# The two score rounds of a key block pair issued together in the middle steps of a four-layer kernel

## The chip, the core and the metric

The kernel runs on one core of a Trainium2 chip. The metric is the device time of one execution in microseconds (us). The times of before are those of 11 runs; the profile is one further execution of the same program, recorded by the hardware profiler.

## The reference, cut to what matters

Four layers are added to x one after another. x has B = 8 sequences of S = 256 tokens of D = 256 numbers. The change concerns the two attention layers, of 16 heads of 16 numbers each.

```python
# layer 0: x = x + (attention and SwiGLU, each behind a conditioned RMS norm)
x = x + _attention(_tc_rmsnorm(x, t, g1w, g1b, b1w, b1b), Wq, Wk, Wv, Wo)
return x + _swiglu(_tc_rmsnorm(x, t, g2w, g2b, b2w, b2b), gate_w, hid_w, out_w)
# attention, in both layer 0 and layer 1 (layer 1 has a mask)
attn = einsum('blhd,bmhd->bhlm', q, k) / scale
p = softmax(attn, axis=-1)
o = einsum('bhlm,bmhd->blhd', p, v)
return o @ Wo.T
# layer 1: attention, RMS norm of its output, a shift and scale from the condition
# layer 2: a quaternion rotation of x3 (in the kernel: products with coefficients)
# layer 3: a mixture of 8 experts, 2 for each token, chosen by a router
```

## The kernel before, in words

All matmuls are fp32, and every instruction of TensorE (PE) stands in the order in which the text of the kernel issues it; in the middle part the instructions of VectorE (DVE) and ScalarE (ACT) do so too (`manual_schedule`). Nothing is moved by a scheduler there.

**Rounds.** `Attention` works on one sequence in one layer. Its heads come in KC = 2 groups c of 8 heads, and the keys in NQ = 2 blocks kc of 128. `scores(c, kc)` (L988) multiplies 4 row tiles of 32 into one score tile `s_a` of 128 x 2048 numbers, and ACT writes its exponential into `pe_a` (L990). `values(c)` (L1001) multiplies both exponentials of a group with the values `va` into `o_a`, in column tiles of 32; DVE then turns and divides the result (`tu_a`, `invs`, `on_a`, `oT_a`, L1010 to L1018). `block()` issues one round: the scores, and then the values of the group whose two exponentials are complete, if one is waiting in `pending`. So an even round (kc = 0) issues scores and values, an odd round (kc = 1) scores alone.

**Pieces.** Between the rounds stand pieces of other work, taken from a generator (`others`), each about 1.7 us of matmuls: the chunks of SwiGLU (`pg`, `ph`, L1128; `pd`, L1141), the projections of the next attention (`pk_a`, `pq_a`, L932; `pv_a`, L954 and L962), transposes (`pt_n`, `pt_x`, L888), and the outward projections (`py`, L1024 and L1174). A `pg` is followed on ACT by the tanh `th` (L1132) and on DVE by `sg` (L1134); a `ph` by `hT` on DVE (L1136); a `pd` reads `hT`.

**PSUM.** The score tile has one buffer, the value tile one, and all the pieces share three:

```python
ps_m = banks.enter_context(tc.tile_pool(name="ps_m", bufs=3, space=PSUM))      # L532
ps_s = last_rounds.enter_context(tc.tile_pool(name="ps_s", bufs=1, space=PSUM))  # L534
ps_o = last_rounds.enter_context(tc.tile_pool(name="ps_o", bufs=1, space=PSUM))  # L535
```

The pieces' buffers are taken in turn: py takes over that of `pg_0`, `ph_2` that of `ph_0`, `pg_4` that of `pg_2`, `ph_4` that of py, and so on. `pe_a` has three buffers.

**Steps.** The loop `for i in range(2, B - 1)` makes five middle steps. Step i calls `run("bbbbbbbb", ...)`: eight rounds, four of layer 1 of sequence i - 2 and four of layer 0 of sequence i + 1, with the pieces of `others(i - 1)`. `run` holds the order: after round t it first starts the generators in `starts[t]`, then takes pieces until the time of `gaps` is spent (in the text's own units), with the outward projection of a finished attention (`then`) among them, and at the end of the round the generators in `beside[t]`. These put work on DVE and ACT: the norms' squares (L878, L1225, ACT) and reciprocal roots (`rsqrt`, L619 to L624, DVE), `xs_n` (L900, ACT), the rotation (L1202, L1207), and, in steps 4 and 6, the routing of a group of two sequences (`route`, L1236 to L1278; `place_choices`). The scores of the next attention read `qz_a` (L946, DVE) and `kT_a` (L942, ACT).

After the loop come the last rounds, with pieces of the first expert tiles, and then the experts by themselves (L1528, L1558).

Of the kernel before, what the change touches and what calls it, by code (L numbers as in the profile page):

```python
# [17 lines left out]
B, S, D = 8, 256, 256  # L18
# [475 lines left out]
def block_kernel(ctx: ExitStack, tc: tile.TileContext, a: dict, out: bass.AP):  # L494
# [372 lines left out]
    def wt(tag, shape, name, bufs=None):  # L867
        return homes.get(tag, work).tile(shape, F32, tag=tag, bufs=bufs or 2, name=name)
# [104 lines left out]
    class Attention:  # L973
# [19 lines left out]
        def values(self, c):  # L993
            va = self.ops[2]
            o = ps_o.tile([P, 2, S], F32, tag="o", name=f"o_{self.name}_{c}")
            for kc in range(NQ):
                pe = self.pes.pop((c, kc))

                for qd in range(2):
                    for i in range(4):  # L1000
                        nc.tensor.matmul(  # L1001
                            o[32 * i : 32 * i + 32, qd, :],
                            va[:, kc, 8 * c + 4 * qd + i].rearrange("p a d -> p (a d)"),
                            pe[:, 2 * qd + i // 2, i % 2, :],
                            start=kc == 0 and qd == 0, stop=kc == NQ - 1 and qd == 1,
                        )


            turned = wt("oS", [P, 2, S // 32, 2, DH], f"tu_{self.name}_{c}")
            nc.vector.transpose(turned.rearrange("p q j a d -> p (q j a d)"), o.rearrange("p q s -> p (q s)"))  # L1010
            inv = invs[:, self.at + c]
            nc.vector.reciprocal(inv, turned[:, :, :, 1, 0])
            on = wt("on", [P, S // 32, 2, DH], f"on_{self.name}_{c}")
            nc.vector.tensor_tensor(
                on.rearrange("p j q d -> p q j d"), turned[:, :, :, 0, :],
                inv.unsqueeze(3).to_broadcast([P, 2, S // 32, DH]), ALU.mult,
            )
            nc.vector.transpose(self.oT[:, c, :], on.rearrange("p j q d -> p (j q d)"))  # L1018
# [13 lines left out]
    def do_deferred():  # L1032
        while deferred:
            for _ in deferred.pop(0):
                pass
# [5 lines left out]
    def in_parts(b, key):  # L1041

        yield from state[b].pop(key)
# [150 lines left out]
    def rotate(b):  # L1194

        g, bi = divmod(b, GB)
        x3 = state[b].pop("x3").rearrange("p t (i c) -> p t i c", c=C)
        x4, raw = groups[g]
        dst = x4[:, bi * NQ : (bi + 1) * NQ, :].rearrange("p t (j c) -> p t j c", c=C)
        for i in range(4):  # L1200
            term = wt("oS", [P, NQ, 4, C], f"term_{b}_{i}") if i else dst
            nc.vector.tensor_tensor(  # L1202
                term, x3[:, :, i, :].unsqueeze(2).to_broadcast([P, NQ, 4, C]),
                coef[:, i].unsqueeze(1).to_broadcast([P, NQ, 4, C]), ALU.mult,
            )
            if i:
                nc.vector.tensor_tensor(dst, dst, term, ALU.add)  # L1207
            if i in (1, 2):
                yield
        if bi == GB - 1:  # L1210
            x4, raw = groups.pop(g)
            for o in (tokens_r, out_r):
                nc.sync.dma_start(out=o[:, g * NTG : (g + 1) * NTG, :], in_=x4)
        yield
        if bi == GB - 1:
            yield from route(g, x4, raw)
# [473 lines left out]
    def block():  # L1690
        layer, b, c, kc = queue.pop(0)
        second = layer == "a1"
        if (c, kc) == (0, 0):
            live[layer, b] = Attention(
                state[b].pop(f"qkv{int(second)}"), f"{layer}_{b}", (2 * b + second) * KC
            )
        live[layer, b].scores(c, kc)
        then = values()
        if second and (c, kc) == (KC - 1, NQ - 1):
            nc.vector.tensor_copy(wo1[:, :, D:], hall[:, :, b, :])  # L1700
        if kc == NQ - 1:
            pending.append((layer, b, c))
        return then

    def run(what, pieces, us=0.0, beside={}, rest=True, owed=None, hold=False, soon=3, late_=(), starts={}):

        spent, due, held = 0.0, 0.0, None
        for t, kind in enumerate(what):
            then = block() if kind == "b" else values() if kind == "v" else None
            do_deferred()
            for g in starts.get(t, ()):
                next(g, None)
            if held:
                held()  # L1720
                spent += 1.9
            held = None
            then, owed = then or owed, None
            if t in late_:
                held, then = then, None
            gap = us if isinstance(us, float) else us[t]
            due = max(due + gap, spent + min(gap, 3.0))
            n = 0
            while spent < due or (then and n < soon):
                w = next(pieces, "end")  # L1730
                if w == "break":
                    due = spent
                if w in ("break", "end"):
                    break
                spent += 1.9 if w is None else w
                n += 1
                if then and n == soon:
                    then()
                    spent += 1.9
                    then = None  # L1740
            if then and hold:
                return then
            if then:
                then()
                spent += 1.9
            for g in beside.get(t, ()):
                next(g, None)
        if rest:
            for _ in pieces:
                pass  # L1750
# [5 lines left out]
    def of(f, b):  # L1756
        return f(b) if 0 <= b < B else iter(())
# [3 lines left out]
    def others(b):  # L1761


        nxt, mine = of(first, b + 3), swiglus.pop(b)
        swiglus[b + 1] = of(swiglu, b + 1)
        n = 0 if b == 0 else 1
        for k, w in enumerate(mine, n):
            yield w
            if k == 0:
                yield "break"  # L1770
            if k == 11:

                yield next(nxt) if b + 3 < B else next(swiglus[b + 1], 0.0)
            if k == 12:
                if b + 3 < B:
                    yield next(nxt)
                    yield next(nxt)
                else:
                    yield "break"
            if k == 13:  # L1780
                if b + 3 < B:
                    yield from nxt
                else:
                    yield "break"
            if k == 14 and b + 3 < B:
                yield next(swiglus[b + 1])

    def once(f, *args):
        f(*args)
        yield  # L1790

    def at_once(*gens):
        for g in gens:
            for _ in g:
                pass
        yield
# [10 lines left out]
    with tc.manual_schedule(engines=by_text):  # L1807
# [35 lines left out]

        operands = first(1)
        run("b", chain(take(1, operands), set_up_condition(), set_up_router(cond_g)), 9.0, rest=False)
        run("b", take(1, operands), 9.0, {0: [once(prepare_quaternions)]}, rest=False)
        n1 = first_norm(2)
        run("b", iter(()), 0.0, {0: [n1]})
        run("b", operands, 9.0, {0: [at_once(n1)]}, rest=False)
        operands = first(2)  # L1850
        then = run("b", iter(()), 0.0, hold=True)
# [23 lines left out]
        gaps = [1.9, 5.0, 7.2, 7.2, 7.2, 7.2]  # L1875
# [5 lines left out]
    for i in range(2, B - 1):  # L1881

        placed = {
            2: lambda: once(compare_queries), 3: lambda: once(set_up_rows), 4: lambda: at_once(place_choices(0)),
            6: lambda: at_once(place_choices(1)),
        }.get(i, lambda: iter(()))()
        last, rotated = rotated, rotate(i - 2)
        n1 = first_turned(i + 2) if i + 2 < B else iter(())
        n2, r1 = in_parts(i, "n2"), in_parts(i - 2, "r1")
        gaps = [7.6, 5.7, 3.8, 5.7, 8.2, 3.8, 2.5, 3.8] if i + 2 < B else [7.6, 3.8, 1.9, 5.7, 7.6, 1.2, 1.9, 3.8]  # L1890
        starts = {0: [last, n1], 1: [last, n2], 2: [n2]}
        beside = {
            0: [last, n1], 1: [last, n2], 2: [n1], 3: [last], 4: [placed], 5: [r1], 6: [rotated],
            7: [rotated, rotated],
        }
        if i == B - 2:

            early = table("early", (NG - 2) * NTG, EARLY, ALU.is_ge)
            beside[4].insert(0, early)
            beside[7].append(early)  # L1900
        run("bbbbbbbb", others(i - 1), gaps, beside, late_=() if i + 2 < B else (4,), starts=starts)


    pieces = others(B - 2)
# [20 lines left out]
    pieces = last  # L1925
# [22 lines left out]
    owed = block()  # L1948
# [162 lines left out]
```

## Time and profile before

| | |
|---|---|
| median of 11 runs | 703.74 us |
| lowest and highest | 702.47 and 706.68 us |
| the profiled execution | 703.11 us |
| its span, first to last instruction | 701.3 us |
| mean granted TensorE clock in it | 0.997 |
| the five middle steps in it | 92.08 to 355.25 us |
| lengths of the steps i = 2 to 6 | 53.16, 53.17, 54.21, 53.17, 49.46 us |
| scores, all 64 rounds | 73.0 us of PE |
| exponentials, 64 | 120.1 us of ACT, 1877 ns each |

A step is counted from the start of its first scores to the start of the next step's first scores. PE's busy time is that of matmuls; PEld is the loading of weights, which runs beside them. In the lists of the chain and the timeline, the first number is the start and the second the length in us, and in square brackets stands the idle time before, with what ended it. An end of a matmul in the profile is modelled, so lengths on PE are best read from start to start.

### The profile page before, as it was taken

Reading aid. Unit: us, or ns where it says so; the run is one execution under the profiler, and the core shown is the slowest. Engines: PE = TensorE matmul, PEld = TensorE weight load, DVE = VectorE, ACT = ScalarE, POOL = GpSimd, SP = SyncE. Lnnn points to the kernel's source line nnn. Section 1 sums busy time; section 2 is a strip of 40 time slices with the busy share of each in tenths; the row PEclk is TensorE's granted clock in tenths of the full one; section 3 lists DMA queues with packets and bytes.
Section 4 is the critical chain, followed back from the end, with each engine's and each line's share of the span. In section 5 each row is a group of like instructions: output and inputs, shape, how many; then the busy total and the mean of one; then the engine's idle time right before and its main releaser. Section 6 shows DMA issues by size and latency. Waiting matters only on the chain.

```text
span 701.3 us, 11187 instructions
## 1 busy us (share of the span) xinstructions
PE 687.1 (98%) x4258; PEld 529.8 (76%) x4258; DVE 365.9 (52%) x1165; ACT 255.6 (36%) x411; POOL 180.5 (26%) x223
## 2 busy tenths in 40 slices
PE   8999999999999999999999999999999999999995
PEld 7567776767666667766666786688888998999894
DVE  4664354584488576477675676688222222222221
ACT  4664243544454444354444235322111222221220
POOL 5501500000000231000320016224373432442213
PEclk9999999999999999999999999999999999999998
DMA  9410101002012000020000051746585866576712
GB/s 294 159 61 16 38 1 38 16 1 39 16 61 39 1 17 8 6 71 1 7 11 1 17 204 20 299 138 208 145 305 163 229 234 189 171 270 190 253 27 29
DMA packets 28879, 70.01 MB, mean 100 GB/s; under 512 B 9033, under 2 KB 22225, under 8 KB 26385
## 3 DMA queue, kind: packets, MB, share of 16 engines
q1 hardware_dynamic: 20032, 57.70, 25.0%
q0 software_dynamic: 8496, 11.32, 7.4%
q8 instruction: 35, 0.57, 0.3%
q14 instruction: 28, 0.22, 0.1%
q10 hardware_dynamic: 288, 0.18, 0.1%
HBM read 59.67 MB, written 9.53 MB: 99 GB/s over the span
## 4 chain that ended last, share of the span: by engine, by line
PE 90%; DVE 5%; ACT 2%; DMA 1%; issue 1%; SPq 0%; POOL 0%; POOLq 0%; DVEq 0%; ACTq 0%
PE ph_a_rest L1528 10%; PE s_a L988 9%; PE pd L1141 8%; PE pg L1128 8%; PE ph_a_p L1528 7%; PE ph L1128 7%; PE o_a L1001 7%; PE ph_s_sure L1528 6%; PE pe_a_rest L1558 3%; PE pq_a L932 3%; PE pk_a L932 3%; PE pe_a_p L1558 3%; PE py L1024 2%; PE pe_s_sure L1558 2%; PE pv_a L954 2%; PE py L1174 2%
## 5 line engine op out<-in xcount | busy, mean ns | idle before, releaser
L990 ACT ACTIVATE pe_a<-s_a 128x2048 f32<-128x2048 f32 x64 | 120.1, 1877 | 101.1 <-PE s_a L988 101.0
L988 PE MATMUL s_a<-qz_a,kT_a 32*128 32x512 f32 x512 | 73.0, 639 | 3.2 <-DVE xg L1159 0.9
L1001 PE MATMUL o_a<-pe_a,va 128*32 128x256 f32 x1024 | 61.9, 382 | 0.0
L1128 PE MATMUL pg<-xT_n,gate_wT 128*128 128x256 f32 x256 | 61.8, 384 | 0.0
L1128 PE MATMUL ph<-xT_n,hid_wT 128*128 128x256 f32 x256 | 61.6, 383 | 0.0
L1001 PEld LDWEIGHTS o_a<-pe_a,va 128*32 128x32 f32 x1024 | 30.0, 109 | 39.9 <-issue 23.4
L1141 PE MATMUL pd<-out_wT,hT 128*128 128x256 f32 x256 | 59.7, 384 | 0.4 <-DVE hT L1136 0.4
L1141 PEld LDWEIGHTS pd<-out_wT,hT 128*128 128x128 f32 x256 | 47.4, 190 | 13.7 <-issue 4.0
L1128 PEld LDWEIGHTS ph<-xT_n,hid_wT 128*128 128x128 f32 x256 | 47.7, 190 | 13.3 <-DVE rq_v_n L619 2.3
L1128 PEld LDWEIGHTS pg<-xT_n,gate_wT 128*128 128x128 f32 x256 | 47.6, 190 | 12.0 <-issue 3.6
L1010 DVE STREAM_TRANSPOSE tu_a<-o_a 128x512 f32<-128x512 f32 x32 | 22.8, 712 | 52.3 <-PE o_a L1001 52.3
L1528 PE MATMUL ph_a_rest<-h_a_rest,w_a_rest 128*128 128x256 f32 x224 | 49.6, 379 | 0.0
L1528 PEld LDWEIGHTS ph_a_rest<-h_a_rest,w_a_rest 128*128 128x128 f32 x224 | 42.0, 190 | 5.4
L1101 POOL TENSOR_TENSOR xy<-y,x 128x512 f32<-128x512 f32 x8 | 10.2, 1271 | 139.3 <-DVE rq_v_r L619 55.0
L1539 DVE TENSOR_SCALAR h_a_rest<-ph_a_rest,w_a_rest 128x256 f32<-128x256 f32 x28 | 13.5, 483 | 57.3 <-PE ph_a_rest L1528 56.3
L1316 POOL DMA_INDIRECT slots<-rec,posi x32 | 31.9, 997 | 22.5 <-issue 7.3
L988 PEld LDWEIGHTS s_a<-qz_a,kT_a 32*128 32x128 f32 x512 | 20.0, 182 | 22.3 <-issue 13.1
L1134 DVE SCALAR_TENSOR_TENSOR sg<-th,pg 128x512 f32<-128x512 f32 x32 | 21.9, 686 | 28.4 <-ACT th L1132 28.3
L1528 PE MATMUL ph_a_p<-h_a_p,w_a_p 128*128 128x192 f32 (+2 forms) x224 | 36.0, 319 | 0.0
L1132 ACT ACTIVATE th<-pg 128x512 f32<-128x512 f32 x32 | 19.0, 594 | 46.4 <-PE pg L1128 46.4
L1537 ACT ACTIVATE h_a_rest<-ph_a_rest,w_a_rest 128x256 f32<-128x256 f32 x28 | 13.3, 475 | 60.6 <-DVE h_a_rest L1539 60.6
L1528 PEld LDWEIGHTS ph_a_p<-h_a_p,w_a_p 128*128 128x128 f32 x224 | 34.9, 191 | 0.1
(351 smaller groups left out, 1176.9 us busy)
## 6 DMA issues: line engine op xcount, KB each, us to landing
w_a_rest<-in_experts SPq DMA_DIRECT2D x7, 2180.0 KB, 9.2
w_a_p<-in_experts SPq DMA_DIRECT2D x7, 2180.0 KB, 9.3
w_s_sure<-in_experts SPq DMA_DIRECT2D x4, 2180.0 KB, 10.0
w_s_early<-in_experts SPq DMA_DIRECT2D x1, 2180.0 KB
mod<-mod_rows SPq DMA_DIRECT2D x8, 256.0 KB, 3.3
tokens<-x SPq DMA_DIRECT2D x4, 512.0 KB, 3.7
out<-x SPq DMA_DIRECT2D x4, 512.0 KB, 4.7
x<-in_x SPq DMA_DIRECT2D x7, 256.0 KB, 2.7
```

The costliest lines, as they stand in the source:

```text
L932: nc.tensor.matmul(pp[:, c, :], w[:, k, c * P : (c + 1) * P], xT[:, k, :], start=k == 0, stop=k == KC - 1)
L988: nc.tensor.matmul(sc[:, j], kT[r, c, kc * P : (kc + 1) * P], qz[r, c], start=True, stop=True)
L990: nc.scalar.activation(pe, sc, AF.Exp)
L1001: nc.tensor.matmul(o[32 * i : 32 * i + 32, qd, :], va[:, kc, 8 * c + 4 * qd + i].rearrange("p a d -> p (a d)"), pe[:, 2 * qd + i // 2, i % ...
L1010: nc.vector.transpose(turned.rearrange("p q j a d -> p (q j a d)"), o.rearrange("p q s -> p (q s)"))
L1128: nc.tensor.matmul(ps[:, j, :], w[:, k, o : o + P], yT[:, k, :], start=k == 0, stop=k == KC - 1)
L1132: nc.scalar.activation(th, pg, AF.Tanh, scale=0.5)
L1134: nc.vector.scalar_tensor_tensor(sg, th, 1.0, pg, ALU.add, ALU.mult)
L1141: nc.tensor.matmul(pd[:, t, :], hT[:, c, t * P : (t + 1) * P], out_w[:, c, :], start=c == 0, stop=c == HID // P - 1)
L1316: sc = nc.gpsimd.indirect_dma_start(out=slots, out_offset=bass.IndirectOffsetOnAxis(ap=posi[:, t : t + 1], axis=0), in_=rec[:, t, :], in_o ...
L1528: nc.tensor.matmul(ph[:, c - c0, 0:many], w[:, o : o + P], src[:, k, 0:many], start=k == 0, stop=k == n_in - 1,)
L1558: nc.tensor.matmul(pos[q][0:p, q, :], h2[:, k, q * p : (q + 1) * p], w[:, o : o + D], start=k == 0, stop=k == MC - 1,)
```

## The change

`run` gets a parameter `pairs`, which the call of the five middle steps sets. With it, an even round issues two blocks at once: the scores of kc = 0, the values that were waiting, and the scores of kc = 1. The odd round issues no block, only its pieces and generators. The first block returns the outward projection that may be due; the second finds nothing waiting and returns nothing. The rounds before and after the five steps keep the old order. No instruction is added or taken away; tiles, buffers and the `gaps` stay.

```diff
-    def run(what, pieces, us=0.0, beside={}, rest=True, owed=None, hold=False, soon=3, late_=(), starts={}):
+    def run(what, pieces, us=0.0, beside={}, rest=True, owed=None, hold=False, soon=3, late_=(), starts={}, pairs=False):
...
         for t, kind in enumerate(what):
-            then = block() if kind == "b" else values() if kind == "v" else None
+            then = None
+            if pairs:
+
+                if t % 2 == 0:
+                    then = block()
+                    block()
+            else:
+                then = block() if kind == "b" else values() if kind == "v" else None
             do_deferred()
...
-        run("bbbbbbbb", others(i - 1), gaps, beside, late_=() if i + 2 < B else (4,), starts=starts)
+        run("bbbbbbbb", others(i - 1), gaps, beside, late_=() if i + 2 < B else (4,), starts=starts, pairs=True)
```

The block of the fourth round of layer 1 also copies 16 columns into `wo1` (L1700, DVE); the copy moves with it.

## The prediction

> **What bounds the kernel now.** I read the page's busy shares and its chain first, then the middle steps by themselves. "Step i" below is the pass of the loop over i; the five passes start with the scores at 92.08, 145.24, 198.41, 252.62 and 305.79 us and end at 355.25.
>
> ```profile
> PE 687.1 (98%) x4258; PEld 529.8 (76%) x4258; DVE 365.9 (52%) x1165; ACT 255.6 (36%) x411; POOL 180.5 (26%) x223
> PE 90%; DVE 5%; ACT 2%; DMA 1%; issue 1%; SPq 0%; POOL 0%; POOLq 0%; DVEq 0%; ACTq 0%
> ```
>
> TensorE is the bound: it is busy 98% and 90% of the chain lies on it. So an edit counts by what it adds to TensorE's own sequence, or by a hole it makes there. The windows of steps 3, 4 and 6 and the waits of PE from 90 to 360 us show how few holes there are:
>
> ```profile
> 145.24:198.41 53.17, 53.15 (x361) 36.80 (x361) 32.01 (x86) 23.95 (x33) 3.63 (x4) 1.00 0.10 18
> 198.41:252.62 54.21, 53.78 (x364) 37.21 (x364) 38.63 (x129) 25.93 (x42) 11.79 (x14) 1.00 0.15 38
> 305.79:355.25 49.46, 48.60 (x342) 33.16 (x343) 36.81 (x120) 24.54 (x37) 10.97 (x11) 1.00 0.10 28
> ```
>
> ```profile
> PE s_a L988 <- DVE xg L1159: 0.9, 1, 0.9
> PE pd L1141 <- DVE hT L1136: 0.4, 1, 0.4
> ```
>
> The columns of the windows are stretch, length, then busy time of PE, PEld, DVE, ACT, POOL. Steps 2, 3 and 5 have no hole (PE busy 53.15 of 53.17). Steps 4 and 6, which carry the routing of a group on DVE (38.6 and 36.8 us of it against 32.0), have the only two: 0.42 us before a pd in step 4, and 0.87 us before the scores at 355.25. There DVE is already level with PE. Read these two places first.
>
> **The pair itself.** The change moves the scores of every odd round ahead of the pieces of its even round, so that scores, values, scores stand together, 4 times a step, 20 times in all. It adds and removes no instruction on any engine. The chain in step 3 shows the old order, and near 432 us a place that already has the new one:
>
> ```profile
> 161.80 1.07 PE s_a L988 x8
> 162.87 1.86 PE o_a L1001 x32
> 164.74 1.93 PE pg L1128 x8
> 166.66 1.73 PE ph L1128 x8
> 168.39 1.07 PE s_a L988 x8
> 169.46 5.38 PE pd L1141 x24
> ...
> 431.21 1.11 PE s_a L988 x8
> ...
> 432.40 1.89 ACT pe_a L990
> 434.29 0.04 issue
> 434.33 1.14 PE s_a L988 x8
> ```
>
> A piece of 8 matmuls takes 1.73, but 1.92 to 1.93 after scores or values: returning to the full array costs 0.19. Old pair: 1.07 + 1.86 + 0.19 + 1.07 + 0.19 = 4.38 us. In the new pair one return (0.19) is gone, but the score tile has one buffer (L534), so the second scores wait for the exponential of the first. That is released by ACT, not by the values: scores start, +1.21 to the exp's start, +1.88, +0.05 = 3.14 between the starts of the two scores, where 1.07 + 1.86 = 2.93 would do. At 431 us it was 434.33 - 431.14 (the timeline's start) = 3.19. New pair: 3.14 to 3.19, + 1.07, + 0.19 = 4.40 to 4.45, so +0.02 to +0.07; I take 0.05. The exp must find ACT free for this: of the 20 even rounds 19 did in the timeline of before, the starts lying 1.20 to 1.27 after those of the scores; the other (346.25, late by 0.36) lies in step 6 and is inside its sum below. One gain: the scores that open a step now wait 0.08 for the last exp of the step before (pv took 2.06 to the next start instead of 1.98); pt_n, pq and pv will lie between. That is -0.08 at four steps.
>
> [...]
>
> **What moves with it.** Of what a score round issues, the copy into wo1 (L1700, 0.16 us of DVE) moves ahead of sg and hT of the third chunk in program order; it reads nothing late, and POOL's wait for DVE before xT_n (L1076) ends over 5 us before pk needs it. DMAs, POOL's and SP's queues keep their order. On ACT the odd exp now stands ahead of the squares, xs_n and the tanh th of its even round; on PE the pieces of two rounds follow one another without scores between. Two kinds of cover go: time for ACT and DVE to empty the three buffers of ps_m, which every piece takes over from the piece three before it, and time for DVE between a piece and its reader.
>
> In steps 2, 3 and 5 the cover is enough. After the second scores (start 0): exp ends 3.09, two squares of n1 1.04, th, sg: the buffer of pg_0 is free at 5.65, and py, which takes it, starts at 1.07 + 1.83 + 1.73 + 1.73 = 6.36. At the step's end qz (1.39) follows pq while pv takes 1.88: 0.3 to spare. pd needs hT_6 2.6 into itself, and it comes about 1.45 in. Nothing is charged beyond the pairs; if one of these failed it would cost a few tenths in each of three steps.
>
> **Step 4.** T is the start of its first scores, 198.41. ACT in this step, timeline of before:
>
> ```profile
> 199.68 1.88 ACT L990 ACTIVATE pe_a<-s_a 128x2048 f32<-128x2048 f32 x1 [0.59 <-PE s_a L988]
> 201.46 0.40 ACT L1225 ACTIVATE junk_r<-x 128x256 f32<-128x256 f32 x1
> 204.14 0.42 ACT L878 ACTIVATE junk_n<-x 128x256 f32<-128x256 f32 x1
> 204.56 0.58 ACT L1132 ACTIVATE th<-pg 128x512 f32<-128x512 f32 x1
> ```
>
> Six squares lie between the exp and th, and sg (205.17, 0.69) empties pg_0 4.30 after the exp's end; py started at 206.63, with 0.8 to spare. After: the second exp ends at T + 3.14 + 1.21 + 1.88 = T + 6.23, pg_0 is empty at T + 10.53, and py, due at T + 3.14 + 6.36 = T + 9.50, waits 1.05. Then y starts at T + 10.55 + 1.93 = T + 12.48, before T + 10.15 (208.56): 2.33 later. From y on DVE ran without a gap through rsqrt, routing, second rsqrt and the transposes of the values to hT_6, which ended at 225.77, T + 27.36. It starts 2.33 later, so ends at T + 29.7. PE, without a wait, reaches pd at T + 25.3 (py ends 12.28; three pieces 5.19; pair 4.3; two pieces 3.56) and the matmul that needs hT_6 at T + 27.9: it waits 1.8, where 0.42 was. pd goes on at T + 29.7, before T + 27.42: **+2.3**. Without the buffer's wait DVE would still start 1.28 later, giving +1.2: the lower end. The second half adds only its two pairs.
>
> **Step 6.** T is 305.79. Only four squares here: pg_0 is empty 3.22 after the exp, T + 9.45, so py does not wait; y starts 1.28 later. DVE is again unbroken from y (315.94) to hT_4 (ends 329.66), whose buffer partner is pd: T + 25.2 against PE's T + 24.3, +0.9. Then the pair of rounds 4 and 5 stands ahead of the rest of pd, which ends at T + 37.0 (before 340.52, T + 34.73), 2.3 later. From there DVE has one chain, x, placement, o, rsqrt, x3, rotation, qz (340.79 to 355.11, 0.8 of it on ACT's squares), and the scores at 355.25 already waited 0.87 for it. The odd scores that used to run beside this chain have left it, so all of it starts 2.3 later: **+2.3**; if the chain had slack after all, only the pairs, +0.2.
>
> **Sum.** 2.3 + 2.3 + 14 other pairs x 0.05 (0.7) - 0.3 = +5.0 us. Everything after 355 us starts from these scores and keeps its own length. The profiled execution took 703.11 us (span 701.3 and 1.8 around it), so 708.1; the median, 703.74, lies 0.6 above it, so 708.7. The eleven runs lie in two groups, 702.47 to 703.74 and 705.81 to 706.68, and the median is the top of the lower one; a median that falls in the upper would be some 2.5 higher.
>
> **Rivals.**
> 1. No difference: DVE and ACT follow the earlier scores and the two chains start no later; then only pairs, 20 x 0.05 - 0.3 = +0.7, 704.4. For it: DVE is busy only 38.6 of 54.2 us in step 4. Against: it is unbroken exactly from y to hT_6.
> 2. Faster: the saved return counts because the second scores do not wait. This needs the exp to end within 2.93 of the first scores' start (3.14 to 3.19 in the rows); then 20 x (4.38 - 4.19) = 3.8 less, and with both holes (1.3) closed 698.7. It decides from an exp 0.21 earlier. Against: 1.21 and 1.88 are the same in nearly all rows.
> 3. Slower still: the buffer waits reach steps 2, 3 and 5 and each pair costs 0.2: 5.0 + 3 x 0.7 + 14 x 0.15 = +9.2, 713. It needs ACT 0.7 later than in the rows of those steps.
>
> **Numbers.** Forecast 0.70, rival 1 0.10, rival 2 0.04, rival 3 0.16. The low ends of the steps, 1.2 + 0.2 + 14 x 0.02 - 0.3 = +1.4, give 705.1; the range goes down to 704.3 to take in rival 1, and up to 712.3, a median in the upper group and most of the way to rival 3. Left out are rival 2 and the larger part of rival 3, some 0.15. A measurement can tell about 0.3%, 2.1 us, here. Slower: forecast less a small part, and rival 3, 0.85; same: rival 1 and that part, 0.11; faster 0.04.
>
> **What would show it.** Right: the chain shows scores, exp, scores 3.14 apart in all five steps; steps 2, 3 and 5 keep 53.1 to 53.5 us; step 4 grows by about 2.3 with waits of py for DVE (sg) near 1 us and of pd for hT near 1.8; step 6 grows by 2.3 with pd waiting for hT_4 and the wait of the next scores for DVE larger than 0.87. Wrong: steps 4 and 6 unchanged, or all five grow alike, or the second scores start 2.93 after the first.

## The result, and the profile after

The median is 707.80 us over 13 runs (707.16 to 711.32), against 703.54 over 50 runs of the kernel before (702.12 to 706.68). The ratio is 1.0060, 95% interval 1.0046 to 1.0075: slower by 4.3 us. The forecast was 708.7, in the range 704.3 to 712.3.

The page after, the busy shares and the chain that ended last:

```profile
PE 685.1 (97%) x4258; PEld 530.6 (75%) x4258; DVE 365.7 (52%) x1165; ACT 256.5 (36%) x411; POOL 180.6 (26%) x223
PE 83%; DVE 7%; ACT 7%; issue 1%; DMA 1%; SPq 0%; POOL 0%; POOLq 0%; DVEq 0%; ACTq 0%
```

No engine's busy time grew by more than 1 us. TensorE is busy 2 us less than before, and the span is 705.7 instead of 701.3. What grew is the part of the chain that lies on other engines: PE 90% to 83%, ACT 2% to 7%, DVE 5% to 7%. ACT's new share is the exponential inside each pair; it need not cost anything, because the values run beside it. DVE's lies in steps 4 and 6 alone. A share of the chain is not a loss by itself: these 2% are some 14 us, and the steps grew by 4.89.

The windows of the five middle steps after (stretch, length, then busy time of PE, PEld, DVE, ACT, POOL, then the granted clock):

```profile
91.46:144.56 53.10, 52.57 (x361) 37.01 (x360) 29.29 (x80) 24.08 (x32) 3.62 (x4) 1.00 0.08 18
144.56:197.66 53.10, 52.57 (x361) 37.02 (x360) 31.99 (x86) 24.09 (x32) 3.63 (x4) 1.00 0.10 18
197.66:254.49 56.83, 53.56 (x366) 37.31 (x365) 38.64 (x129) 26.27 (x41) 10.87 (x12) 1.00 0.13 36
254.49:307.59 53.10, 52.56 (x362) 37.01 (x361) 31.84 (x84) 24.09 (x32) 5.15 (x9) 1.00 0.05 9
307.59:359.52 51.93, 48.79 (x343) 33.22 (x342) 37.52 (x119) 24.43 (x36) 10.88 (x10) 1.00 0.08 26
```

Steps 2, 3 and 5 are 0.06 to 0.07 us shorter than before (53.16, 53.17, 53.17), step 4 is 2.62 longer (54.21) and step 6 is 2.47 longer (49.46): +4.89 in all. Granted clock 1.00 in each, so the clock is no part of it. The profiled execution also reached its first middle step 0.62 earlier and took some 0.1 longer behind the last, and 4.89 - 0.62 + 0.1 is the 4.4 by which its span grew.

The waits of PE in these steps after (engine, line, waited for: us in total, times, longest):

```profile
PE pd L1141 <- DVE hT L1136: 2.6, 2, 1.7
PE s_a L988 <- ACT pe_a L990: 1.2, 1, 1.2
PE py L1024 <- DVE sg L1134: 1.0, 1, 1.0
PE s_a L988 <- DVE qz_a L946: 0.4, 1, 0.4
PE py L1174 <- DVE count_early L1364: 0.3, 1, 0.3
```

Before there were two waits, 0.9 and 0.4 us. Where these stand shows the timeline of PE after; the first three lines are a pair in step 2, the next three step 4, the others step 6 and the scores behind it:

```profile
91.46 1.14 PE L988 MATMUL s_a<-qz_a,kT_a 32*128 32x512 f32 x8
92.53 1.93 PE L1001 MATMUL o_a<-pe_a,va 128*32 128x256 f32 x32
94.60 1.14 PE L988 MATMUL s_a<-qz_a,kT_a 32*128 32x512 f32 x8
...
208.31 1.99 PE L1024 MATMUL py<-L_WoT_turned,oT_a 128*128 128x256 f32 x8 [0.98 <-DVE sg L1134]
...
223.18 2.75 PE L1141 MATMUL pd<-out_wT,hT 128*128 128x256 f32 x12
...
227.68 2.86 PE L1141 MATMUL pd<-out_wT,hT 128*128 128x256 f32 x12 [1.75 <-DVE hT L1136]
...
333.03 1.99 PE L1141 MATMUL pd<-out_wT,hT 128*128 128x256 f32 x8 [0.85 <-DVE hT L1136]
...
352.56 1.14 PE L988 MATMUL s_a<-qz_a,kT_a 32*128 32x512 f32 x8 [1.23 <-ACT pe_a L990]
...
359.52 1.14 PE L988 MATMUL s_a<-qz_a,kT_a 32*128 32x512 f32 x8 [0.40 <-DVE qz_a L946]
```

Scores to scores 94.60 - 91.46 = 3.14. In step 4, py waits for the buffer that sg has not emptied, and 19 us later pd waits for an hT that is that much late. On ACT the reason stands in order, timeline of ACT after, step 4 (two of the six squares, which are four L1225 and two L878):

```profile
202.07 1.88 ACT L990 ACTIVATE pe_a<-s_a 128x2048 f32<-128x2048 f32 x1 [1.32 <-PE s_a L988]
203.85 0.41 ACT L1225 ACTIVATE junk_r<-x 128x256 f32<-128x256 f32 x1
...
206.54 0.42 ACT L878 ACTIVATE junk_n<-x 128x256 f32<-128x256 f32 x1
206.96 1.06 ACT L1132 ACTIVATE th<-pg 128x512 f32<-128x512 f32 x2
```

The odd exponential, then six squares, then th. Before, the odd scores and their exponential came one round later, and th ended before py was due.

### The profile page after: what moved, and what is told of

It reads as the page before. It is cut to its first block, busy times and chain, and to the rows that moved or that the text cites. A ratio compares the mean times of both kernels' runs of the same rounds, so it can differ in the third digit from the quotient of the medians.

```text
span 705.7 us, 11185 instructions
## 1 busy us (share of the span) xinstructions
PE 685.1 (97%) x4258; PEld 530.6 (75%) x4258; DVE 365.7 (52%) x1165; ACT 256.5 (36%) x411; POOL 180.6 (26%) x223
## 4 chain that ended last, share of the span: by engine, by line
PE 83%; DVE 7%; ACT 7%; issue 1%; DMA 1%; SPq 0%; POOL 0%; POOLq 0%; DVEq 0%; ACTq 0%
PE ph_a_rest L1528 10%; PE s_a L988 9%; PE pd L1141 8%; PE ph_a_p L1528 7%; PE pg L1128 7%; PE ph L1128 6%; PE ph_s_sure L1528 6%; ACT pe_a L990 6%; PE pe_a_rest L1558 3%; PE pq_a L932 3%; PE pk_a L932 3%; PE pe_a_p L1558 3%; PE o_a L1001 3%; PE py L1024 2%; PE pe_s_sure L1558 2%; PE py L1174 2%
## 5 line engine op out<-in xcount | busy, mean ns | idle before, releaser
L946 DVE TENSOR_SCALAR qz_a<-pq_a,par 128x512 f32<-128x512 f32 x32 | 22.5, 746 | 21.3 <-PE pq_a L932 21.3
```

Of the source, the lines that this page charges most:

```text
L946: nc.vector.tensor_scalar(qz[:, :, j, :], pq, par[:, j : j + 1], None, ALU.mult)
```

## The experiments

The theories on trial. **Lost cover:** the pair costs next to nothing by itself; the odd scores were TensorE work that gave ACT and DVE time at certain places, and the loss arises only where DVE has an unbroken chain, in steps 4 and 6. Its rival, **spread:** each pair costs some tenths in all steps. Beside them stands a question of size, **the buffer:** does the second scores' wait on the score tile eat a gain that the pair would have?

Experiments 1 to 3 give `pairs` a set of rounds in place of a yes or no, so that a step or half a step can keep the old order:

```diff
-            if pairs:
+            if t - t % 2 in pairs:
                 if t % 2 == 0:
                     then = block()
                     block()
```

The call of the five steps gives `pairs=range(0, 8) if i in (2, 3, 5) else ()` in experiment 1, `(0, 2)` in 2 and `(4, 6)` in 3.

**1. Pairs in steps 2, 3 and 5 only.**

> Pairs only in steps 2, 3 and 5; steps 4 and 6 in the old order. Theory (the loss is cover lost in the two routing steps): steps 2, 3 and 5 take 53.1 us as with all pairs, steps 4 and 6 54.2 and 49.5 as before, and the time is that of before within 0.1% (703.2 to 703.7, some 0.2 less than before). Rival (each pair costs its share, 4.3 us over 20): 12 pairs cost 2.6 us, ratio 1.0037.

Measured: 53.10, 53.10, 54.22, 53.17, 49.45 us for the five steps (before: 53.16, 53.17, 54.21, 53.17, 49.46). Median 702.87 us over 12 runs against 703.46 over 17, ratio 0.9992 (0.9971 to 1.0013). Twelve of the twenty pairs cost nothing that can be seen, and the spread theory falls. Step 5 lacks the 0.07 that steps 2 and 3 gain. Its first pair stands 3.13 us behind the odd scores of the unpaired step 4, and ACT is still at their exponential when the scores that open step 5 are due; the timeline of PE:

```profile
251.75 1.14 PE L988 MATMUL s_a<-qz_a,kT_a 32*128 32x512 f32 x8
252.82 1.94 PE L1001 MATMUL o_a<-pe_a,va 128*32 128x256 f32 x32
254.96 1.14 PE L988 MATMUL s_a<-qz_a,kT_a 32*128 32x512 f32 x8 [0.20 <-ACT pe_a L990]
```

254.96 - 251.75 is 3.21 instead of 3.14: the scores at 251.75 had to wait for the buffer themselves, and their exponential starts 1.27 behind them (253.02) instead of 1.21. At 434.33 before it was 1.26 (432.40 - 431.14), hence 3.19. Why the exponential starts later there no run shows.

**2 and 3. Pairs in rounds 0 to 3 only, and in rounds 4 to 7 only, in all five steps.**

> Only rounds 0 to 3 of each step are paired. Theory: step 4 keeps all of its loss (56.8 us: py waits about 1.0 for sg, pd about 1.75 for hT_6), step 6 about 1.0 of it (50.4 to 50.5: y 1.3 later, pd waits about 0.85 for hT_4, and the scores at the end wait about 0.9 for DVE as before), steps 2, 3 and 5 stay at 53.1. Sum about +3.5 us. Rival (the loss is spread over the pairs): half of it in each step, step 4 55.5, step 6 50.7.

> Only rounds 4 to 7 of each step are paired. Theory: step 4 takes 54.1 to 54.3, no loss at all; step 6 loses the cover that the odd scores of round 5 gave to the DVE chain behind pd: 1.3 to 1.5 us, so 50.8 to 51.0; steps 2, 3 and 5 53.1. With the kernel that pairs rounds 0 to 3 the two losses of step 6 add up to the 2.5 of all pairs. Rival (spread): step 4 55.5, step 6 50.7.

Measured, the steps in order: for rounds 0 to 3, 53.17, 53.24, 56.88, 53.24, 50.81; for rounds 4 to 7, 53.10, 53.09, 54.22, 53.09, 50.63. Step 4 is one place: +2.67 with the early pairs, +0.01 with the late ones. Step 6 is two: +1.35 and +1.17, together 2.52, the 2.47 of the whole change. I had expected the early part of it at 50.4 to 50.5 and the late part at 50.8 to 51.0, so the division was off by 0.2 to 0.4, the sum was not. The timeline of PE in the kernel with rounds 0 to 3 paired, step 6 and the scores behind it:

```profile
336.89 2.00 PE L1141 MATMUL pd<-out_wT,hT 128*128 128x256 f32 x8 [0.84 <-DVE hT L1136]
...
362.20 1.14 PE L988 MATMUL s_a<-qz_a,kT_a 32*128 32x512 f32 x8 [0.85 <-DVE xg L1159]
```

The early pairs make pd wait for hT_4, and the last wait stays at 0.85, the 0.87 of before: the whole of DVE's chain has only moved. (Single times, here 710.06 and 706.94 us, are not compared for experiments 2 to 6, but the lengths of the steps; the last section gives the reason.)

**4. Without the buffer's wait.** The exponential of the even round of each pair is taken over the first half of the scores only, and the values use that half for all heads.

```diff
-            nc.scalar.activation(pe, sc, AF.Exp)
+            n = 2 if half[0] else 4
+            nc.scalar.activation(pe[:, 0:n], sc[:, 0:n], AF.Exp)
...
-                            pe[:, 2 * qd + i // 2, i % 2, :],
+                            pe[:, (0 if (c, kc) in self.short else 2 * qd) + i // 2, i % 2, :],
```

> All pairs, but the exponential of each even round of the five steps is taken of the first half of the score tile only (128 x 1024), and the values of that key block use that half for all eight heads; the second half is left out. This asks what the new order would give if the second scores did not wait for the score buffer. Theory (it is the exp that they wait for, and one return to the full array is saved): the starts of the two scores lie 2.93 apart instead of 3.14, set by the values, and steps 2, 3 and 5 take 53.10 - 4 x 0.21 = 52.3 us. Rival (going from values to scores costs a change of its own, hidden until now behind the exp): 3.0 to 3.1 apart, 52.6 to 53.0 us. The time at the end is not to be compared, since the router may choose other experts.

The chain in step 2 of this kernel (start, length, what), and its exponential in the timeline of ACT:

```profile
95.28 1.07 PE s_a L991 x8
96.35 1.86 PE o_a L1006 x32
98.21 1.07 PE s_a L991 x8
99.28 1.92 PE pg L1133 x8
```

```profile
96.42 1.02 ACT L994 ACTIVATE pe_a<-s_a 128x1024 f32<-128x1024 f32 x1 [0.57 <-PE s_a L991]
```

The exponential takes 1.02 instead of 1.88, and the second scores start 2.93 after the first, straight behind the values. The chain now stays on PE. Steps 2, 3 and 5 are 52.29 us, 0.81 shorter than with the whole exponential: 0.20 a pair. So the gain that rival 2 wanted exists, and the one buffer takes it. It would not have saved the change: steps 2, 3 and 5 are 0.88 shorter than in the kernel before, and by that measure step 4 should be 53.33 and step 6 48.58. They are 56.21 and 51.53, 2.9 us longer each, where the same reckoning gives 2.7 and 2.5 for the change itself. So the loss of cover does not come from the buffer's wait.

**5. All pairs, the squares behind the first th.** In round 0 the generators of `starts` run after the first piece instead of before it.

```diff
-            for g in starts.get(t, ()):
-                next(g, None)
+            later = list(starts.get(t, ()))
+            if not (pairs and t == 0):
+                while later:
+                    next(later.pop(0), None)
...
+                while later:
+                    next(later.pop(0), None)
```

> All pairs; in round 0 of each step the squares of the routing and of n1 are issued on ACT behind the tanh of the first piece instead of ahead of it. Theory (th stood behind six squares, so pg_0 was emptied late and py, and with it the whole DVE chain, started late): the wait of py for sg goes from 0.98 to 0, y starts 1.25 earlier, hT_6 ends as much earlier, and step 4 goes from 56.83 to 55.5 to 55.7; pd still waits about 1.8, since PE comes to it earlier too. Rival (the DVE chain of the routing alone sets step 4, and py's wait is hidden in front of it): the step stays at 56.8 and pd's wait grows to 2.7.

Measured: step 4 55.58 us, 1.25 less than with the change alone; steps 2, 3 and 5 as with it (53.11, 53.10, 53.10); step 6 51.77, 0.16 less. The timeline of PE, step 4:

```profile
207.69 1.89 PE L1024 MATMUL py<-L_WoT_turned,oT_a 128*128 128x256 f32 x8
...
226.97 2.86 PE L1141 MATMUL pd<-out_wT,hT 128*128 128x256 f32 x12 [1.76 <-DVE hT L1136]
```

py no longer waits, so the squares ahead of th are the cause of that wait. pd waits as long as before: py, pd's due time and DVE's chain from y all came some 1.2 to 1.3 earlier. The two waits of step 4 are two terms, not one seen twice.

**6. All pairs, the routing of steps 4 and 6 moved to the end of round 3.**

```diff
+        routing = i in (4, 6)
+        if routing:
+            starts = {0: [n1], 1: [n2], 2: [n2]}
...
+        if routing:
+            beside[0], beside[1], beside[3] = [n1], [n2], [last] * 6
```

> All pairs; in steps 4 and 6 the four parts of the routing (squares, reciprocal root, choices, counts) are issued together at the end of round 3, behind hT_6, instead of in rounds 0, 1 and 3. Theory (the routing on DVE between y and hT is what made the lost cover visible): neither py nor pd waits, step 4 takes 53.6 to 53.8 (56.83 - 1.1 - 1.75 - 0.3, with the placement's two small matmuls in it), step 6 51.0 to 51.3, as the chain behind pd stays. Rival (the pieces stand too close in any case): the waits of py and pd stay in part, step 4 above 55.

Measured: step 4 53.56 us (3.27 less than with the change alone, and 0.65 less than before it), step 6 50.71 (1.22 less, where 0.6 to 0.9 less was expected). All waits of PE in the five steps:

```profile
PE s_a L988 <- ACT pe_a L990: 1.3, 1, 1.3
PE s_a L988 <- DVE qz_a L946: 0.4, 1, 0.4
PE py L1174 <- DVE count_early L1364: 0.3, 1, 0.3
```

The waits of py for sg and of pd for hT are gone, with all pairs in place. They hung on where the routing stands in DVE's and ACT's order. What is left lies in the second half of step 6: the chain of x, placement, o, x3, rotation and qz.

**7 and 8. That chain moved too, with the pairs and without them.** To the edit of experiment 6 this adds, in step 6, the placement at the end of round 6 and the rotation at the end of round 7; 8 has both edits on the kernel before.

```diff
         if i == B - 2:
...
+            beside[4], beside[6], beside[7] = [], [placed], [rotated, rotated, rotated]
```

> As the kernel with the routing later, and in step 6 the placement moves from round 4 to round 6 and all three parts of the rotation to round 7, behind qz. All pairs. Theory (all of the loss is cover, the pair itself costs nothing): steps 2, 3 and 5 53.1, step 4 53.7, step 6 48.7 to 49.3, in all some 1.2 less than before: ratio 0.998 to 0.999. Rival (the pair itself costs something that shows only in full): ratio above 1.002.

> The same moves of routing, placement and rotation in the kernel of before, without any pairs. Theory: the two holes of before close, 0.42 in step 4 (53.8) and 0.87 in step 6 (48.6); steps 2, 3 and 5 stay at 53.17; 1.3 less than before, ratio 0.998. So with and without pairs come out alike within 0.1%. Rival: if pairs carry a gain or a loss of their own, this kernel and the one with pairs differ by 20 times it.

Measured with the pairs: 53.10, 53.11, 53.55, 53.11, 48.65 us, sum 261.52; without: 53.17, 53.16, 53.54, 53.16, 48.43, sum 261.46. PE has no wait in either between 92 us and the end of the steps. Medians 702.23 us (12 runs) and 702.37 (12 runs), ratios of the means to the kernel before (23 runs) 0.9974 (0.9958 to 0.9991) and 0.9974 (0.9955 to 0.9992). Part of that is the mix of runs: 9 of the 23 runs of before lie in the upper of the two groups of the last section, and 1 and 2 of these 12. The medians of the lower groups are 703.31, 702.13 and 702.17, ratio 0.998. With DVE's two chains out of the way the pairs, which cost 4.9 us in the change, cost 0.06. That is lost cover in one comparison, and both versions beat both kernels. Steps 4 and 6 came out 0.05 to 0.3 shorter than expected. Of the 1.7 us that the steps gain on 263.17, 0.8 is given back in the first round after them, which takes 10.83 us to the next scores instead of 10.04, because PE waits for sg there (timeline of PE, 7):

```profile
353.62 1.14 PE L988 MATMUL s_a<-qz_a,kT_a 32*128 32x512 f32 x8
...
362.53 1.99 PE L1024 MATMUL py<-L_WoT_turned,oT_a 128*128 128x256 f32 x8 [0.53 <-DVE sg L1134]
```

## Why the prediction was right, point by point

- **The pair** (forecast: S to S 3.14, each pair +0.02 to +0.07, the start of a step -0.08). S to S was 3.13 to 3.15 in 19 of 20 pairs. The cost was over-sized: with four pairs the steps came out 0.06 to 0.07 shorter, where 4 x 0.05 - 0.08 = +0.12 was forecast. With the -0.08 taken as it stands, a pair costs 0.00 to 0.01. The pv that ends a step takes 1.87 to the next scores where it took 2.06; 0.10 of that it gains because it no longer stands behind scores (pieces take 1.83 from start to start behind tiled matmuls and 1.73 behind other pieces), which the pair's sum counts already, and the other 0.09 is the forecast 0.08. Over the twenty pairs this term was some 0.8 to 1.0 too high.
- **The return that is saved** (forecast: 0.19 a pair, read from the trace as 1.92 against 1.73, and taken by the buffer's wait). In experiment 4, where the second scores stand straight behind the values, 2.93 from the first, a pair took 0.20 us less than with the whole exponential. In the change itself the buffer's wait decided, 3.14, as the row at 431 us said.
- **Step 4** (forecast +2.3; py waits 1.05, y at T + 12.48, hT_6 ends at T + 29.7, pd waits 1.8). With T = 197.66: py waited 0.98, y started at T + 12.68, hT_6 ended at T + 29.97, pd waited 1.75; the step grew by 2.62. Each link held, 0.1 to 0.3 late: py started at T + 10.65 instead of 10.55, y 2.03 behind it instead of 1.93, and DVE took 17.29 from y to the end of hT_6 where it took 17.21. That makes the 0.3 by which the step was under-sized. The timeline of DVE, three rows before and the same three after:

```profile
205.17 0.69 DVE L1134 SCALAR_TENSOR_TENSOR sg<-th,pg 128x512 f32<-128x512 f32 x1 [1.36 <-ACT th L1132]
...
208.56 0.69 DVE L1100 TENSOR_TENSOR y<-py,x 128x512 f32<-128x512 f32 x1 [0.41 <-PE py L1024]
...
225.08 0.69 DVE L1136 TENSOR_TENSOR hT<-sg,ph 128x512 f32<-128x512 f32 x1
```

```profile
207.56 0.69 DVE L1134 SCALAR_TENSOR_TENSOR sg<-th,pg 128x512 f32<-128x512 f32 x1 [3.58 <-ACT th L1132]
...
210.34 0.69 DVE L1100 TENSOR_TENSOR y<-py,x 128x512 f32<-128x512 f32 x1 [0.70 <-PE py L1024]
...
226.94 0.69 DVE L1136 TENSOR_TENSOR hT<-sg,ph 128x512 f32<-128x512 f32 x1
```

- **Step 6** (forecast +2.3: no wait of py, pd for hT_4 +0.9, the end of pd and DVE's chain to qz 2.3 later). pd waited 0.85; with T = 307.59, x started at T + 37.57 where it was T + 35.00, so 2.57 later; the step grew by 2.47. py waited a little after all: sg emptied the buffer at 317.09 and py started at 317.15, T + 9.56 instead of T + 9.50, and took 1.83 instead of 1.73, as it also did behind its wait in step 4. With the squares later (experiment 5) neither is there, and the step is 0.16 shorter. The timeline of DVE, x before and after:

```profile
340.79 0.69 DVE L1147 SCALAR_TENSOR_TENSOR x<-pd,xy 128x512 f32<-128x512 f32 x1 [0.73 <-PE pd L1141]
```

```profile
345.16 0.69 DVE L1147 SCALAR_TENSOR_TENSOR x<-pd,xy 128x512 f32<-128x512 f32 x1 [0.73 <-PE pd L1141]
```

- **One step was wrong.** I said that the scores behind step 6 would wait for DVE longer than the 0.87 of before. They waited 0.40. PE lost time earlier in two waits that I had not seen: 1.23 us of the odd scores of round 6 for the even exponential, and 0.27 of py (L1174). The timeline of ACT after, step 6:

```profile
349.20 0.42 ACT L878 ACTIVATE junk_r<-o 128x256 f32<-128x256 f32 x1 [7.84 <-DVE o L1175]
...
350.16 0.57 ACT L1154 COPY x2T<-pt_x 128x512 f32<-128x512 f32 x1
350.62 1.88 ACT L990 ACTIVATE pe_a<-s_a 128x2048 f32<-128x2048 f32 x1
```

The scores of round 6 start at 348.32, and the exponential, due 1.21 later at 349.53, starts at 350.62. It stands on ACT behind x2T and the squares of o, for the first of which ACT had waited 7.84 us, on DVE. So the late DVE chain reached PE at three places: at py, which waited for `count_early` right behind x, by way of ACT and the score buffer, and directly by qz. The prediction failed here by naming one place where the chain meets PE and not the two others on its way. The time was not missed, because all of these places hang on the same chain, and its end was forecast.
- **The sum.** Forecast 2.3 + 2.3 + 0.7 - 0.3 = +5.0; measured 2.62 + 2.47 - 0.20 (steps 2, 3 and 5) = +4.89. Two errors nearly cancel: steps 4 and 6 were 0.5 too low, the pairs and the starts of the steps 0.6 too high. That the sum came within 0.1 is luck; that the terms of steps 4 and 6 came within some 0.3 of theirs is not. Of the 0.9 between 708.7 and 707.80, 0.1 lies in the steps and 0.5 ahead of and behind them in the two profiled executions; the other 0.3 is the step from one execution to the median, 0.6 in the forecast and 0.27 after (707.80 over 707.53).
- **The rivals.** Rival 1 (the chains start no later) falls with the waits of py and pd. Rival 2's gain exists and is taken by the buffer (experiment 4). Rival 3 (all steps) falls with experiment 1.

## What to carry to other kernels

A block of matmuls between two pieces may be another engine's time. Before moving it, look along the path for an engine that is lightly used on average but has one stretch without a gap, and ask what that stretch starts from: here DVE, 52% busy, decided 4.9 us in two places, and moving its chains by a round made the order of the scores a matter of 0.06 us. And where two users of one buffer are put side by side, count from release to release (3.14), not the work on the engine in front (2.93).

## What was unexpected of the hardware

The times of every version that ran several times lie in two groups, their medians 3.0 to 3.6 us apart. Before: 35 of 50 from 702.12 to 704.18 and 15 from 705.81 to 706.68; after: 11 of 13 up to 709.02 and two at 711.00 and 711.32. The medians of the lower groups are 702.93 and 707.78, 4.85 apart, which is the 4.89 of the steps. The ten traces fall in two groups as well, and show where they part: within the first 14 us. The timeline of PE at the start, of the kernel after and then of experiment 3:

```profile
7.82 0.60 PE L914 MATMUL pt_n<-ident,xs_n 128*128 128x128 f32 x4
8.26 0.61 PE L1811 MATMUL unread<-ident 128*128 128x128 f32 x4
8.84 1.99 PE L932 MATMUL pk_a<-xT_n,L_WkT 128*128 128x256 f32 x8
```

```profile
10.59 1.06 PE L914 MATMUL pt_n<-ident,xs_n 128*128 128x128 f32 x4
11.44 1.06 PE L1810 MATMUL unread<-ident 128*128 128x128 f32 x4
12.29 2.59 PE L932 MATMUL pk_a<-xT_n,L_WkT 128*128 128x256 f32 x8
```

Four matmuls of 128 x 128 take 0.44 us from start to start in the one (8.26 - 7.82) and 0.85 in the other (11.44 - 10.59): half the rate, and it stays so into pk_a; the first scores then start at 18.27 instead of 14.76. The trace's first record of a granted clock, 1.00, stands at 4.60 us in the kernel after and at 13.71 in experiment 3; a window ahead of it prints 1.00 too, but without a record. Experiments 2, 3, 4 and 6 had their profiled execution in the late group (first record at 13.46 to 14.16 us, first middle step at 94.9 to 95.2), the others and the two kernels in the early one (4.33 to 6.25, and 91.3 to 92.1). That is why single times were not compared here, and the lengths of the steps were. The late group keeps the low rate for some 12 us in which PE's timeline has no gap (1.50 to 13.71 in experiment 3): there the first 18 matmuls of 128 x 128 take 4.14 us from start to start (5.64 - 1.50), 0.23 each, and the 16 matmuls of 8 columns behind them 3.51 (9.15 - 5.64), where the kernel after takes 1.88 (7.05 - 5.17). What puts an execution in one group or the other no run here shows.
